# Two-layer attention on one core: the residual update moved to the next even block, four units between the layers, both group means in odd blocks

## The chip, the cores and the metric

The kernel runs on one core of a Trainium2 chip. The metric is the device time of one execution in microseconds (us), from the first to the last instruction. The engines are named as in the profile: PE is TensorE, the matrix engine (PEld is its weight load), DVE is VectorE, ACT is ScalarE, POOL is GpSimd, SP is SyncE, which here only issues DMA transfers. [...]

## The reference

Two layers, both of the same form, over x of shape (16, 256, 32, 32): a group norm, then attention with four heads over 1024 positions, then a residual.

```python
def layer(x, Wq, bq, Wk, bk, Wv, bv, rel_h, rel_w):     # heads 4, d 64, n 1024
    xf = gn(x).reshape(b, c, n)          # mean and variance over groups of the last axis
    q, k, v = proj(Wq, bq), proj(Wk, bk), proj(Wv, bv)
    sim  = einsum('bhdi,bhdj->bhij', q, k)
    qpos = einsum('hdi,bhdj->bhij', (rel_h + rel_w).reshape(heads, d, n), q)
    attn = softmax(sim + qpos, axis=-1)
    return x + einsum('bhdn,bhmn->bhdm', v, attn).reshape(b, c, w, h)
```

The norm of layer 1 reads the x that layer 0 has updated, so the two layers of one batch depend on each other; different batches do not.

## The kernel before

**Units and blocks.** A unit is one layer of one batch; there are 32, and the list `units` (L139 to L142) sets their order. Before the change the layer-1 unit of a batch follows its layer-0 unit by three to five places. A unit is cut into four blocks, by pair of heads `pr` (0, 1) and by half of the queries `half` (0, 1). In this text b0, b1, b2, b3 are the four blocks of a unit; b0 and b2 are **even** (`half` is 0), b1 and b3 are **odd**. There are 128 blocks, 31 units and the first two blocks of the last going through `block` (L621) and the last two through `block_without_pieces` (L747).

**One block.** For each of eight tiles j of 128 keys: DVE writes the position term of the scores into PSUM (`seed`, L343), PE adds the products of k and q to it (`scores`, L379), ACT takes the exponential into `p` in SBUF (L388). DVE adds up the tiles 0 to 6 of `p` into `acc` (`add_up`, L397 and L399); tile 7 is added by an accumulating DMA from POOL's queue (`add_last`, L430). PE multiplies `p` with the values in two stretches (`attend`, L413) into `po`, and ACT copies `po` to `od` (`take_out`, L488). Between the score tiles PE makes the projections for the coming blocks (`prepare`, L262, L292, L320). PSUM holds four buffers of this size, whose roles are in `ring`; a seed needs the buffer that an earlier exponential, copy or mean has been read out of.

**Tokens.** A product of two stretches has a dependence between them that PE is told of through POOL: POOL waits for the last matmul of the first stretch, writes `token` (L163), and PE's second stretch waits for it. `x.word()` places this write in POOL's queue.

**Softmax sums.** The `acc` of a block is folded by DMA: `add_last`, then `fold` (L435, POOL's queue, 256 KB accumulating), then `stack_up` (L444, SP's queue), then `fold_again` (L451, POOL). PE sums the stack at the end of the next even block (L463), ACT copies the sums out (L478), and two transfers on SP's queue bring them to `den_all` (L484).

**The residual of a pair.** `reciprocals` (L515) waits for `den_all`, takes the reciprocal on DVE (L522), writes it to DRAM (`rd`, L524) and reads it back spread over 64 partitions each (`rden`, L529), both on SP's queue. `finish` (L534) multiplies `od` by `rden` (L541), adds bias and x (L543), both on DVE, and in layer 1 stores x (L545). Before the change both stand in the same odd block: `reciprocals` after score tile 4, `finish` behind the first stretch of `attend` and ahead of the seeds 1 to 3 of the block that follows. `load_x` (two transfers of 512 KB for a later batch, L106) stands near the start of b3, ahead of both on SP's queue.

**The norm of a later unit.** ACT takes the group sums of unit u+2 (`norm_sums`, 16 instructions), then PE the mean over rows (`norm_mean`, L207), then ACT the sums of squares (`norm_squares`, 16), PE their mean (`norm_var`), POOL the reciprocal root (L231), and in the next unit ACT normalises (`norm_apply`, 16). Before the change the sums lie in b1 and b2, the mean in b2, the squares in b2 and b3, the second mean in b3, and the normalisation in b0 (15) and b1 (1). A mean needs a PSUM buffer, `f1`, zeroed by DVE (L199) and read by ACT before the next seed can use it.

Of the kernel before, what the change touches and what calls it, by code (L numbers as in the profile page):

```python
# [19 lines left out]
G = 16  # L20
# [32 lines left out]
def fast_path(ctx, tc, sh, x, layers, out, W, den_all, token, good, flag):  # L53
# [49 lines left out]
    def load_x(b):  # L103
        xt[b] = xpool.tile([P, CC, N], F32, tag="x", name=f"x_{b}")
        for cc in range(CC):
            nc.sync.dma_start(xt[b][:, cc, :], flat(x[b, cc * P : (cc + 1) * P]))  # L106
# [29 lines left out]
            nc.scalar.copy(w.rearrange("p a c -> p (a c)"), raw_t.pop((l, part)))  # L136


    units = [(b, 0) for b in range(3)]  # L139
    for b in range(3, B):  # L140
        units += [(b - 3, 1), (b, 0)]
    units += [(b, 1) for b in range(B - 3, B)]  # L142
    NU = len(units)
    ks, qs, abt, vts, xns = {}, {}, {}, {}, {}
# [46 lines left out]
    def norm_sums(u, gs):  # L191
        if u not in reds:
            reds[u] = small.tile([P, G], F32, tag="red", name=f"red_{u}")
        for g in gs:
            of_group(u, g, AF.Identity, reds[u])
# [26 lines left out]
    def norm_squares(u, gs):  # L222
        for g in gs:
            of_group(u, g, AF.Square, sums[u], bias=negs[u][:, g : g + 1])
# [14 lines left out]
    def norm_apply(u, gs):  # L239
        rstd, shift = rss[u]  # L240
        for g in gs:
            nc.scalar.activation(  # L242
                grouped(xns[u], g),
                grouped(xt[units[u][0]], g),
                AF.Identity,
                bias=shift[:, g : g + 1],
                scale=rstd[:, g : g + 1],
            )
# [142 lines left out]
    def add_up(blk, j):  # L391
        u, pr, half = blk
        if j == 0:
            return
        if j == 1:
            accs[blk] = apool.tile([P, 2, HALF], F32, tag="acc", name=f"acc_{u}_{pr}_{half}")
            nc.vector.tensor_tensor(accs[blk], probs[blk, 0], probs[blk, 1], ALU.add)  # L397
        else:
            nc.vector.tensor_tensor(accs[blk], accs[blk], probs[blk, j], ALU.add)  # L399
# [221 lines left out]
    def block(n):  # L621
        blk = blocks[n]
        u, b = divmod(n, BPU)
        half = blk[2]
        before = blocks[n - 3][:2] if half == 1 and n > 2 else None
        after = blocks[n + 1] if n + 1 < len(blocks) else None
        previous = blocks[n - 1] if n > 0 else None
        one, two = u + 1 < NU, u + 2 < NU

        pieces = u + 1 < NU or b < 2  # L630
        if u + 1 == NU and b == 1:
            widen(u, 1)
        f0, f1, f2, f3 = ring
        folded = n - 1 < FOLDED
        if not pieces:
            return block_without_pieces(n, half)

        if previous:
            add_up(previous, 6)
            if folded:  # L640
                add_last(previous)
            else:
                add_up(previous, 7)
        for j in range(1, 4):
            scores(blk, j)
        if b == 3 and u + 3 < NU and units[u + 3][0] not in xt:
            load_x(units[u + 3][0])
        (first, first_out), (second, second_out) = prepare(u, b)
        first(0)
        if b == 0 and one:  # L650
            norm_apply(u + 1, range(0, 1))
        if b == 2 and two:
            norm_sums(u + 2, range(8, 11))
        if b == 3 and two:
            norm_squares(u + 2, range(6, 9))
        seed(blk, 4, f1)
        scores(blk, 4)
        add_up(blk, 1)
        if before:
            reciprocals(*before)  # L660
        if b == 0 and one:
            norm_apply(u + 1, range(1, 5))
        if b == 1 and one:
            norm_apply(u + 1, range(15, G))
        if b == 2 and two:
            norm_sums(u + 2, range(11, G))
        if b == 3 and two:
            norm_squares(u + 2, range(9, 11))
        second(0)
        if half == 1:  # L670
            second_out()
        first.word()
        if previous and folded:
            fold(previous)
            stack_up(previous)
        first(1)
        first_out()
        seed(blk, 5, f0)
        scores(blk, 5)
        add_up(blk, 2)  # L680
        if half == 0:
            second.word()
            if previous and folded:
                fold_again(previous)
            second(1)
            second_out()
        seed(blk, 6, f1)
        scores(blk, 6)
        if half == 0:
            ring[2:] = f3, f2  # L690
        seed(blk, 7, ring[2])
        scores(blk, 7)
        add_up(blk, 3)
        add_up(blk, 4)

        if after:
            seed(after, 0, f0)
        if n in check:
            next(checks)
        if b == 0 and one:  # L700
            norm_apply(u + 1, range(5, 10))
        if b == 3 and two:
            norm_squares(u + 2, range(11, G))
        po = psum2(ring[3], f"po_{n}")
        values_of_p = attend(blk, po)
        values_of_p(0)
        if two and b >= 2:
            mean, mean_out = (norm_mean if b == 2 else norm_var)(u + 2, zeroed(f1, f"pm_{n}"))
            mean(0)
        if after:  # L710
            scores(after, 0)
        values_of_p.word()
        if two and b >= 2:
            mean(1)
        if previous and folded and half == 1:
            fold_again(previous)
        if two and b >= 2:
            mean_out()
        add_up(blk, 5)
        if before:  # L720
            finish(*before)
        if after:
            for j in range(1, 4):
                seed(after, j, ring[j % 3])
        if b == 0 and one:
            norm_apply(u + 1, range(10, 15))
        if b == 1 and two:
            norm_sums(u + 2, range(0, 8))
        if b == 2 and two:
            norm_squares(u + 2, range(0, 6))  # L730
        values_of_p(1)
        if half == 1:
            take_out(blk, po)
            pos[n] = po
            return
        if n > 1:
            sums_of_pair(*blocks[n - 2][:2], po)
        take_out(blk, po, n > 1)
# [8 lines left out]
    def block_without_pieces(n, half):  # L747

        blk = blocks[n]
        u, pr, _ = blk  # L750
        f0, f1, f2, f3 = ring
        before = blocks[n - 2][:2] if half == 0 else (u, pr)
        first = index[before + (0,)]
        if half == 0:
            add_up(blocks[n - 1], 6)
        add_up(blocks[n - 1], 7)
        for j in range(1, 4):
            scores(blk, j)
        sums_of_p(blocks[first:n], pos[n - 1])
        keep_sums(outs[before], pos[n - 1], first, n - first)  # L760
        add_up(blk, 1)
        seed(blk, 7, f2)
        add_up(blk, 2)
        add_up(blk, 3)
        for j, tag in ((4, f1), (5, f0), (6, f1)):
            scores(blk, j, tag)
        reciprocals(*before, n - first)
        scores(blk, 7)
        add_up(blk, 4)
        if half == 0:  # L770
            seed(blocks[n + 1], 0, f0)
        po = pos[n] = psum2(f3, f"po_{n}")
        values_of_p = attend(blk, po)
        values_of_p(0)
        if half == 0:
            scores(blocks[n + 1], 0)
        if half == 0:
            seed(blocks[n + 1], 1, f1)
            seed(blocks[n + 1], 2, f2)
        add_up(blk, 5)  # L780
        if half == 0:
            seed(blocks[n + 1], 3, f0)
        add_up(blk, 6)
        if half == 0:
            finish(*before)
            values_of_p(1)
            take_out(blk, po)
            return
        add_up(blk, 7)
        acc = accs.pop(blk)  # L790
        pd = psum2(f0, "pd")
        sums_on_rows(acc, pd)
        values_of_p(1)
        finish_half(u, pr, 0, outs[u, pr][:, 0, :], rdens[u, pr][:, :HALF])
        rden = rdens[u, pr][:, HALF:]
        nc.vector.reciprocal(rden, pd[:, 0, :])
        pd = psum2(f2, "pd_columns")[:, 0, : 2 * HALF // P]
        sums_on_columns(acc, pd)
        finish_half(u, pr, 1, po[:, :, :QUART], rden)
        list(in_range(flatden[:, 8 * checked : 8 * n], 1))  # L800
        list(in_range(pd, 2))
        nc.vector.tensor_reduce(good[:, 3:4], good[:, 0:3], AX.X, ALU.min)
        pc = psum2(f1, "pc")[0:1, 0, 0:1]
        nc.tensor.matmul(pc, good[:, 3:4], W.ones[:, 0:1], start=True, stop=True)
        nc.vector.tensor_copy(flag, pc)
# [410 lines left out]
```

## Time and profile before

Three runs took 2679.92, 2682.69 and 2690.53 us; the median is 2682.69 us. The profiled execution has a span of 2682.0 us at a granted TensorE clock of 0.994.

| group of instructions | count | mean ns | what it is |
|---|---|---|---|
| DVE L343 | 1018 | 1228 | seed of one score tile |
| DVE L399, L397 | 644, 128 | 1218 | adding one tile to `acc` |
| DVE L541, L543 | 63, 63 | 1221, 1285 | the two halves of `finish` |
| ACT L388 | 1024 | 1117 | exponential of one tile |
| ACT L187 of `x` | 480 | 309 | one group's sum |
| ACT L187 of `x,neg` | 498 | 410 | one group's squares |
| ACT L242 | 496 | 496 | normalising one group |
| POOL L430 to landing | 124 | 4.7 us | tile 7 added by DMA, 512 KB |
| POOL L435 to landing | 124 | 3.6 us | `fold`, 256 KB |

The busy times say which engine is full on the average; the waits say which other engine or transfer an engine stood still for; the timeline, which lists the instructions in order of time, says where in a block it happened. A bracket such as [3.77 <-DMA rden<-rd] gives the idle time of that engine just before the instruction and what ended it.

The length of a block can be read off the timeline of ACT: it is the distance from the start of one block's exponential of tile 1 to the next block's. Over the units 2 to 28:

| block | mean us | shortest us |
|---|---|---|
| b0 | 22.29 | 21.21 |
| b1 | 18.83 | 18.04 |
| b2 | 21.76 | 21.50 |
| b3 | 19.94 | 18.52 |
| a unit | 82.82 | |

The first block's mark is at 33.52 us and the last block's at 2654.44 us, so 127 block lengths make up 2620.92 us of the span.

### The profile page before, as it was taken

How to read it: one execution, taken by the hardware profiler on the slowest of the kernel's cores; microseconds unless marked ns; L12 is line 12 of the kernel's file. 1: busy time of each engine (PE TensorE's matmuls, PEld its weight loads, DVE VectorE, ACT ScalarE, POOL GpSimd, SP SyncE). 2: the span in 40 equal slices, each digit the busy share in tenths (PEclk: the TensorE clock that was granted, in tenths of full speed). 3: DMA queues.
4: the chain of work that ended last, by engine and by line, in shares of the span. 5: the costliest groups of instructions: out<-in, count | busy, mean ns of one | idle time of the engine just before them, and what ended most of it. 6: DMA issues, size and time to landing. Idle time of an engine off the chain costs nothing.

```text
span 2682.0 us, 86789 instructions
## 1 busy us (share of the span) xinstructions
PE 2595.6 (97%) x37970; PEld 1410.4 (53%) x37970; DVE 2261.4 (84%) x2076; ACT 1986.3 (74%) x3996; POOL 565.7 (21%) x949
## 2 busy tenths in 40 slices
PE   8999999999999999999999999999999999999998
PEld 4555455554555555555545555455554555555555
DVE  7888888888888888888888888888888888889888
ACT  6777777777777777777777778777786777777754
POOL 1221222212222122222222221222212222122210
PEclk9999999999999999999999999999999999999999
DMA  3343343433434334343343333433334333333331
GB/s 88 59 83 64 70 90 70 92 68 69 97 67 90 75 59 103 69 85 75 70 91 71 83 75 79 84 69 80 81 75 85 66 82 81 70 75 73 79 75 46
DMA packets 93994, 205.30 MB, mean 77 GB/s; under 512 B 35880, under 2 KB 37416, under 8 KB 93608
## 3 DMA queue, kind: packets, MB, share of 16 engines
q0 software_dynamic: 39680, 113.80, 25.2%
q1 hardware_dynamic: 53928, 85.89, 11.5%
q8 instruction: 299, 4.90, 0.8%
q14 instruction: 87, 0.71, 0.1%
HBM read 51.78 MB, written 17.30 MB: 26 GB/s over the span
## 4 chain that ended last, share of the span: by engine, by line
PE 61%; DMA 16%; DVE 10%; issue 5%; ACT 4%; POOL 2%; SPq 1%; DVEq 0%; POOLq 0%
PE po L413 26%; PE ps L379 19%; PE pq L262 7%; DMA den_all<-od 6%; DVE ps L343 5%; PE pk L262 4%; PE pv L292 4%; DMA rd<-r 4%; DMA rden<-rd 4%; ACT p L388 2%; DVE acc L399 1%; ACT od L488 1%; DVE acc L397 1%; ACT junk L187 1%; PE po L463 1%
## 5 line engine op out<-in xcount | busy, mean ns | idle before, releaser
L343 DVE TENSOR_TENSOR ps<-abt 128x1024 f32<-128x1024 f32 x1018 | 1225.8, 1228 | 317.3 <-ACT p L388 123.2
L388 ACT ACTIVATE p<-ps,shift 128x1024 f32<-128x1024 f32 x1024 | 1102.3, 1117 | 432.3 <-PE ps L379 304.3
L379 PE MATMUL ps<-q,k 64*64 64x512 f32 x8192 | 1033.3, 600 | 48.6 <-DVE ps L343 45.6
L413 PE MATMUL po<-p,v 64*64 64x256 f32 x16384 | 933.1, 376 | 2.4 <-POOL token L163 2.4
L413 PEld LDWEIGHTS po<-p,v 64*64 64x64 f32 x16384 | 658.7, 133 | 306.8 <-issue 58.8
L399 DVE TENSOR_TENSOR acc<-acc,p 128x1024 f32<-128x1024 f32 x644 | 784.4, 1218 | 5.3 <-ACT p L388 0.5
L379 PEld LDWEIGHTS ps<-q,k 64*64 64x64 f32 x8192 | 313.4, 133 | 480.9 <-DVE ps L343 258.4
L451 POOL DMA_DIRECT2D stack<-acc x248 | 195.2, 874 | 450.6 <-DMA stack<-acc 424.1
L262 PE MATMUL pq<-xn,Wq 64*64 64x512 f32 x2048 | 244.6, 593 | 9.6 <-POOL token L163 9.2
L292 PE MATMUL pv<-Wv,xn 64*64 64x256 f32 x4096 | 247.6, 376 | 0.5 <-DVE var L864 0.3
L262 PE MATMUL pk<-xn,Wk 64*64 64x512 f32 x2048 | 243.2, 590 | 4.7 <-POOL token L163 4.6
L430 POOL DMA_DIRECT2D acc<-p x124 | 111.9, 903 | 536.9 <-ACT p L388 360.6
L292 PEld LDWEIGHTS pv<-Wv,xn 64*64 64x64 f32 x4096 | 176.6, 134 | 84.1 <-issue 51.5
L242 ACT ACTIVATE xn<-x,nshift,rstd 128x128 f32<-128x128 f32 x496 | 210.3, 496 | 3.7 <-POOL nshift L233 3.6
L163 POOL MEMSET token<- 1x1 f32 x380 | 50.8, 134 | 704.2 <-PE po L413 474.5
L187 ACT ACTIVATE junk<-x,neg 128x128 f32<-128x128 f32 x498 | 196.9, 410 | 1.0
L435 POOL DMA_DIRECT2D acc<-acc x124 | 101.9, 822 | 396.8 <-DMA acc<-p 387.2
L262 PEld LDWEIGHTS pq<-xn,Wq 64*64 64x64 f32 x2048 | 76.9, 134 | 155.6 <-issue 119.1
L397 DVE TENSOR_TENSOR acc<-p,p 128x1024 f32<-128x1024 f32 x128 | 155.9, 1218 | 0.0
L187 ACT ACTIVATE junk<-x 128x128 f32<-128x128 f32 x480 | 144.5, 309 | 1.0 <-DVE x L543 1.0
L262 PEld LDWEIGHTS pk<-xn,Wk 64*64 64x64 f32 x2048 | 73.9, 133 | 132.0 <-issue 102.8
L488 ACT COPY od<-po 128x512 f32<-128x512 f32 x127 | 74.7, 589 | 75.0 <-PE po L413 75.0
(79 smaller groups left out, 1173.5 us busy)
## 6 DMA issues: line engine op xcount, KB each, us to landing
acc<-p POOLq DMA_DIRECT2D x124, 512.0 KB, 4.7
rden<-rd SPq DMA_DIRECT2D x126, 256.0 KB
acc<-acc POOLq DMA_DIRECT2D x124, 256.0 KB, 3.6
x<-in_x_dram SPq DMA_DIRECT2D x32, 512.0 KB
stack<-acc SPq DMA_DIRECT2D x248, 64.0 KB
stack<-acc POOLq DMA_DIRECT2D x248, 64.0 KB, 2.6
out_dram<-x SPq DMA_DIRECT2D x31, 512.0 KB
den_all<-od SPq DMA_DIRECT2D x124, 4.0 KB
```

The lines of the kernel that those rows point to most:

```text
L187: nc.scalar.activation(junk, grouped(xt[units[u][0]], g), func, accum_out=into[:, g : g + 1], **bias)
L242: nc.scalar.activation(grouped(xns[u], g), grouped(xt[units[u][0]], g), AF.Identity, bias=shift[:, g : g + 1], scale=rstd[:, g : g + 1],)
L262: yield nc.tensor.matmul(pk[c, nh, :], w[l][rs, cc, c0 : c0 + D], xns[u][rs, cc, nh * HALF : (nh + 1) * HALF], start=(t == 0 and cc == 0), ...
L292: yield nc.tensor.matmul(pv[c, a, i, :], xns[u][rs, cc, j0 : j0 + D], W.wv[l][rs, cc, :], start=(t == 0 and cc == 0 and i == 0), stop=(t = ...
L343: nc.vector.tensor_tensor(ps.rearrange("p h (w y) -> p h w y", y=H), ab[:, :, :H].unsqueeze(2).to_broadcast([P, 2, XH, H]), ab[:, :, H + h ...
L379: nc.tensor.matmul(ps[c, h, :], a[hs, j0 : j0 + D], b[hs, columns], start=bool(tag) and i == 0, stop=i == len(terms) - 1, skip_group_check ...
L388: nc.scalar.activation(p, ps, AF.Exp, bias=W.shift)
L397: nc.vector.tensor_tensor(accs[blk], probs[blk, 0], probs[blk, 1], ALU.add)
L399: nc.vector.tensor_tensor(accs[blk], accs[blk], probs[blk, j], ALU.add)
L413: yield nc.tensor.matmul(po[c, a, :QUART], vts[u][rs, j, c0 : c0 + D], p[rs, h, a * QUART : (a + 1) * QUART], start=(t == 0 and j == 0), s ...
L430: nc.gpsimd.dma_start(accs[blk], probs[blk, NT - 1], accum_op=ALU.add)
L451: nc.gpsimd.dma_start(stacks[u, pr][r0 : r0 + R, :], acc[R:D, h, :], accum_op=ALU.add)
```

## The change

`finish` leaves the odd block in which its `reciprocals` stands and goes to the next even block, ahead of the first stretch of `attend`. `reciprocals` stays in the odd block, but moves from behind tile 4 to behind tile 5. `load_x` moves behind both and behind `stack_up` in b3. In exchange DVE's sixth addition of an odd block moves from the next block's start to its own end. In even blocks the token write of the second projection moves ahead of `fold`.

Layer 1 of a batch may then not start as early, so the order of units is changed: four layer-0 units first, and at least four units between the layers of a batch. This lets the group sums of unit u+2 start in b0; the mean is then taken in b1 and that of the squares in b3, both odd, all 16 squares in b2, and the normalisation is split over b0 (9) and b1 (7). The purpose is to give the round trip of the reciprocals a block's time more, and to share the work of DVE and ACT out more evenly between even and odd blocks.

```diff
-    units = [(b, 0) for b in range(3)]
-    for b in range(3, B):
-        units += [(b - 3, 1), (b, 0)]
+    units = [(b, 0) for b in range(4)] + [(0, 1), (1, 1)]
+    for b in range(4, B - 1):
+        units += [(b, 0), (b - 2, 1)]
+    units.insert(-1, (B - 1, 0))
     units += [(b, 1) for b in range(B - 3, B)]
...
-        before = blocks[n - 3][:2] if half == 1 and n > 2 else None
+        summed = blocks[n - 3][:2] if half == 1 and n > 2 else None
+        before = blocks[n - 4][:2] if half == 0 and n > 3 else None
...
         if previous:
-            add_up(previous, 6)
+            if half == 1:
+                add_up(previous, 6)
...
-        if b == 3 and u + 3 < NU and units[u + 3][0] not in xt:
-            load_x(units[u + 3][0])
...
         add_up(blk, 1)
-        if before:
-            reciprocals(*before)
...
         first.word()
+        if half == 0:
+            second.word()
         if previous and folded:
             fold(previous)
-            stack_up(previous)
         first(1)
         first_out()
         seed(blk, 5, f0)
         scores(blk, 5)
+        if summed:
+            reciprocals(*summed)
+        if previous and folded:
+            stack_up(previous)
+            if half == 0:
+                fold_again(previous)
+        if b == 3 and u + 3 < NU and units[u + 3][0] not in xt:
+            load_x(units[u + 3][0])
         add_up(blk, 2)
         if half == 0:
-            second.word()
-            if previous and folded:
-                fold_again(previous)
             second(1)
...
         if after:
             seed(after, 0, f0)
+        if before:
+            finish(*before)
...
-        if two and b >= 2:
-            mean, mean_out = (norm_mean if b == 2 else norm_var)(u + 2, zeroed(f1, f"pm_{n}"))
+        if two and half == 1:
+            mean, mean_out = (norm_mean if b == 1 else norm_var)(u + 2, zeroed(f1, f"pm_{n}"))
...
         add_up(blk, 5)
-        if before:
-            finish(*before)
+        if half == 1:
+            add_up(blk, 6)
         if after:
             for j in range(1, 4):
                 seed(after, j, ring[j % 3])
```

The places of the norm's instructions in a block, by the count in each:

| | b0 | b1 | b2 | b3 |
|---|---|---|---|---|
| before | 15 normalising | 1 normalising, 8 sums | 8 sums, 6 squares | 10 squares |
| after | 9 normalising, 9 sums | 7 normalising, 7 sums | 16 squares | none |

In the last two blocks the residuals move on in the same way: the even one finishes the pair before the last but one, and the last block takes over one more `finish`, near its start.

More of the change, by code (lines that the diff above doesn't have):

```diff
@@ L651, in block @@
             norm_apply(u + 1, range(0, 1))
[L652 to L655, printed above, removed]
+        if b == 1 and two:
+            norm_sums(u + 2, range(9, 11))
         seed(blk, 4, f1)
@@ L658, in block @@
         add_up(blk, 1)
-        if before:
-            reciprocals(*before)
         if b == 0 and one:
             norm_apply(u + 1, range(1, 5))
-        if b == 1 and one:
-            norm_apply(u + 1, range(15, G))
+        if b == 1 and two:
+            norm_sums(u + 2, range(11, 12))
         if b == 2 and two:
-            norm_sums(u + 2, range(11, G))
-        if b == 3 and two:
-            norm_squares(u + 2, range(9, 11))
+            norm_squares(u + 2, range(0, 5))
         second(0)
@@ L700, in block @@
         if b == 0 and one:
-            norm_apply(u + 1, range(5, 10))
-        if b == 3 and two:
-            norm_squares(u + 2, range(11, G))
+            norm_apply(u + 1, range(5, 9))
+        if b == 0 and two:
+            norm_sums(u + 2, range(0, 2))
+        if b == 1 and two:
+            norm_sums(u + 2, range(12, G))
+        if b == 1 and one:
+            norm_apply(u + 1, range(9, 11))
+        if b == 2 and two:
+            norm_squares(u + 2, range(5, 11))
         po = psum2(ring[3], f"po_{n}")
@@ L712, in block @@
         values_of_p.word()
-        if two and b >= 2:
+        if two and half == 1:
             mean(1)
@@ L716, in block @@
             fold_again(previous)
-        if two and b >= 2:
+        if two and half == 1:
             mean_out()
         add_up(blk, 5)
-        if before:
-            finish(*before)
+        if half == 1:
+            add_up(blk, 6)
         if after:
@@ L724, in block @@
                 seed(after, j, ring[j % 3])
[L725 to L728, printed above, removed]
+        if b == 0 and two:
+            norm_sums(u + 2, range(2, 9))
+        if b == 1 and one:
+            norm_apply(u + 1, range(11, G))
         if b == 2 and two:
-            norm_squares(u + 2, range(0, 6))
+            norm_squares(u + 2, range(11, G))
         values_of_p(1)
@@ L751, in block_without_pieces @@
         f0, f1, f2, f3 = ring
[L752 to L755, printed above, removed]
+        summed = blocks[n - 2][:2] if half == 0 else (u, pr)
+        before = blocks[n - 4][:2] if half == 0 else blocks[n - 3][:2]
+        first = index[summed + (0,)]
         add_up(blocks[n - 1], 7)
@@ L759, in block_without_pieces @@
         sums_of_p(blocks[first:n], pos[n - 1])
-        keep_sums(outs[before], pos[n - 1], first, n - first)
+        keep_sums(outs[summed], pos[n - 1], first, n - first)
+        if half == 1:
+            finish(*before)
         add_up(blk, 1)
@@ L766, in block_without_pieces @@
             scores(blk, j, tag)
-        reciprocals(*before, n - first)
+        reciprocals(*summed, n - first)
         scores(blk, 7)
@@ L775, in block_without_pieces @@
         if half == 0:
+            finish(*before)
             scores(blocks[n + 1], 0)
@@ L784, in block_without_pieces @@
         if half == 0:
-            finish(*before)
             values_of_p(1)
```

## Prediction

> **What bounds the kernel now.** I read the busy shares first, then the waits, then the timeline of one unit.
>
> ```profile
> PE 2595.6 (97%) x37970; PEld 1410.4 (53%) x37970; DVE 2261.4 (84%) x2076; ACT 1986.3 (74%) x3996; POOL 565.7 (21%) x949
> ```
>
> PE is taken all the time and DVE has 16% left, so PE sets the pace and DVE is the first candidate to hold it up. That PE is 97% busy doesn't mean that only 3% can be gained: where PE is fed well, three score tiles take 2.75 us (timeline, 882.32), where their seeds come late the same 24 matmuls are shown as busy for 4.70 us (859.26). The block lengths measure this better. The shortest b0, b1, b2 and b3 add up to 21.21 + 18.04 + 21.50 + 18.52 = 79.27 us, the mean unit takes 82.82. So 3.55 us a unit, or 110 over 31 units, are stalls of some kind. The waits name them:
>
> ```profile
> DVE ps L343 <- ACT neg L217: 92.1, 30, 4.0
> ...
> DVE od L541 <- DMA rden<-rd: 53.6, 20, 4.5
> ...
> PEld pq L262 <- POOL token L163: 24.0, 25, 2.8
> ...
> DVE r L522 <- DMA den_all<-od: 22.1, 28, 1.7
> ...
> PEld pm L207 <- ACT junk L187: 15.5, 30, 0.5
> ```
>
> Columns: total us, times, longest. The largest is harmless: DVE waits 3 us in b2 for the buffer of the mean, but PE runs its second stretch meanwhile and goes on without a gap at 837.58. The second is not, as this timeline of one b3 shows:
>
> ```profile
> 839.67 0.90 SPq L106 DMA_DIRECT2D x<-in_x_dram  x2
> ...
> 842.52 0.33 SPq L524 DMA_DIRECT2D rd<-r  x1
> ...
> 849.13 1.16 SPq L529 DMA_DIRECT2D rden<-rd  x2
> ...
> 855.52 1.23 DVE L541 TENSOR_TENSOR od<-od,rden 128x1024 f32<-128x1024 f32 x1 [3.77 <-DMA rden<-rd]
> 856.78 1.28 DVE L543 SCALAR_TENSOR_TENSOR x<-od,bv,x 128x1024 f32<-128x1024 f32 x1
> 857.98 3.52 DVE L343 TENSOR_TENSOR ps<-abt 128x1024 f32<-128x1024 f32 x3
> ...
> 859.26 3.14 PE L379 MATMUL ps<-q,k 64*64 64x512 f32 x16 [2.85 <-DVE ps L343]
> ```
>
> A load of x goes out, the round trip of the reciprocals takes 842.5 to 855.5, 13 us, DVE stands at `finish`, the seeds behind it come late, and PE stops. Without a load (888.05) the round trip makes it in time for 897.12. In the 13 b3 from unit 1 to 25 that have the load (the odd units) the block takes 21.35 us on the mean, against 18.53 in the undisturbed ones.
>
> The third wait is in b0:
>
> ```profile
> 1027.52 0.93 POOL L430 DMA_DIRECT2D acc<-p  x1 [1.38 <-DVE acc L399]
> ...
> 1034.54 0.83 POOL L435 DMA_DIRECT2D acc<-acc  x1 [5.41 <-DMA acc<-p]
> 1035.06 0.33 POOL L163 MEMSET token<- 1x1 f32 x1
> ...
> 1035.44 1.09 PE L262 MATMUL pq<-xn,Wq 64*64 64x512 f32 x8 [1.35 <-POOL token L163]
> ```
>
> The token for PE stands in POOL's queue behind `fold`, and `fold` waits for `add_last` to land. PE's q projection was ready and waited for a memset.
>
> [...] the rows L399 and L541 show 1218 and 1221. Back to back they start 1.13 to 1.15 us apart in the timeline, so I count 1.14 each. [...] beside the load of 839.67 `fold` can go 8.9 us after its `add_last` (840.36 to 849.23), without one 4.9 (882.75 to 887.63).
>
> **The change, part by part.** No arithmetic is added or removed; only places change.
>
> 1. `finish` a block later. Its data has then landed 15 us and more before (a round trip of 9 us from 888, against a `finish` that comes in the second half of the next block), instead of up to 4.5 us late, and the 53.6 us of DVE waits vanish. What it is worth to PE: b3 with the load falls by 21.35 − 18.53 = 2.8 us, 13 times, **37 us**. The late seeds also start the next b0 late (b0 after such a b3 takes 22.66 us, after the others 21.87); that is part of item 2.
>
> 2. Tokens ahead of `fold`, and an earlier `add_last`: the sixth addition of an odd block no longer waits behind three seeds of the next. b0 should come from 22.29 to about its shortest, 21.25: 1.04 × 31 = **32 us**. Nothing queued behind loses: `fold` waits for `add_last` longer than for either product.
>
> 3. `reciprocals` behind tile 5. At 887.77 DVE stood 0.73 us for `den_all` between two seeds, and PE then waited for tile 6 (891.47). One seed, 1.14 us, now fills this; longest wait so far 1.7. b1 would go from 18.83 to 18.04, but it takes over the mean: eight tiny matmuls, and the four sums in front of it end about when they are needed (exponential of tile 7 ends some 1.7 us into the stretch, 4 × 0.30 us of sums, stretch 3.45). I take 18.4: 0.43 × 31 = **13 us**.
>
> 4. The means. b2 loses one: 21.76 to 21.35, **13 us**, most of which is jitter passed on from b3. b3 keeps one but no squares in front of it, so the 0.52 us that PE waits for ACT (15.5 in the list) go: 18.53 to 18.1, 0.43 × 31 = **13 us**.
>
> 5. DVE's load by block, at 1.14 us an operation: even 5 additions + 8 seeds + 2.4 for `finish` = 17.2 of 21.3 us; odd 7 additions + 8 seeds + 0.3 = 17.4 of 18.2. Before: 15.96 and 18.7. I followed the queue through a pair with the buffer releases: in even blocks the last seed ends 1.1 us before PE needs it; in odd ones, after the buffer of tile 1 is free at 2.3 us, seed 6 ends at 8.25 where PE comes for it at 8.6. It fits, barely. Cost 0; bounded above by one addition, 1.14 us, in each of 63 odd blocks, 72 us.
>
> 6. ACT, at the timeline's 0.41 us for a normalisation, 0.30 a sum, 0.40 a square: b0 6.15 to 6.4 us, b1 2.8 to 5.0, b2 4.8 to 6.4, b3 4.0 to 0. The additions in b1 and b2 lie beside the stretches of `attend`, where ACT waits 3.20 us (898.07) and 3.02 (833.94) for PE. Cost 0; upper bound 4.05 us a unit.
>
> 7. `load_x` now runs across the end of b3; before, it stretched the `add_last` of the same block, and the next is 7 us away. Free, or up to the 1.2 us left when `add_last` lands 3.8 us later (8.5 us, its median in the odd units' b3, against 4.7) and the slack of `fold_again` before the next token (2.6 us at 877.9) is used up.
>
> 8. The order of units by itself computes the same. The last block gets a `finish`: 2.4 us of DVE under at least 10 us of PE work; I take +1.5.
>
> Sum, by block lengths, which also take in the small jitter of b3 in even units (18.88 on the mean): a unit at 21.25 + 18.4 + 21.35 + 18.1 = 79.1 us. Such sums never quite come in, since the queue of item 5 has half a microsecond of play; I add 0.6. 31 units at 79.7 and three blocks at 57.9 make 2528.6 us in place of 2620.9: −92.3 + 1.5, from 2682.7 to **2592**.
>
> **The rivals.**
>
> *A, the DMA contention only moves.* The store of x now goes out at the end of even blocks, just ahead of `den_all`, and the load just ahead of b0's `add_last`. For it: the round trip above shows how much a load can stretch others. Against: it has its 7 us. Price: item 7's 1.2 × 12, and a `den_all` 0.4 us too late in 62 odd blocks: 39 us, **2631**.
>
> *B, DVE becomes the bound in odd blocks.* For it: 17.4 of 18.2 us. Against: b1 had 18.7 us of DVE before and did 18.04 when nothing was late. Price 72 us: **2664**.
>
> *C, ACT pays.* The added norm work in b0 to b2 delays the exponentials and thus the buffers for the seeds, and what leaves b3 gains nothing: +4.05 us a unit against a gain of 3.1, × 31 = +29: **2712**. Against: the 3 us gaps of item 6.
>
> **How the numbers follow.** Forecast 0.70, A 0.16, B 0.08, C 0.06. Low end: no allowance and both odd blocks at 18.04 give 78.7 a unit, 2560; high end: A and a little more, 2634. Outside lie B, C and a little of the rest. Faster by over 0.5% (under 2669): the forecast, A and most of B, 0.92; within 0.5% 0.03; slower 0.05.
>
> **What would show it.** L541 has no wait for `rden` left; pq and pk no longer wait for tokens behind L435; b3 of odd units is as short as that of even ones (under 18.5 us) and b0 under 21.6. B would show as PE waiting for L343 at tiles 6 and 7 of odd blocks with DVE free of waits; A as waits of L522 for `den_all` or of PE for tokens behind L451; C as L343 waiting for L388 for much more than 123 us. The forecast is wrong if the stalls of b0 stay although the tokens come early: then something else than POOL made them.

## The result, and the profile after

The changed kernel takes 2569.01 us (median of 4 runs, 2566.68 to 2572.34), the kernel before 2686.61 (4 runs, 2679.92 to 2692.4). The ratio is 0.9564, 95% interval 0.9535 to 0.9593: 4.4% or about 117 us faster. The forecast was 2592, its range 2560 to 2634.

The page of the changed kernel, its first part, to be held against the line of before in the prediction:

```profile
PE 2542.5 (99%) x37970; PEld 1634.3 (64%) x37970; DVE 2260.2 (88%) x2076; ACT 1980.4 (77%) x3996; POOL 567.8 (22%) x949
```

The counts in this line are the same, and DVE is busy for the same 2260 us; only the span around it has shrunk. The chain that ended last, by engine, says it better than PE's 97 and 99%. Before:

```profile
PE 61%; DMA 16%; DVE 10%; issue 5%; ACT 4%; POOL 2%; SPq 1%; DVEq 0%; POOLq 0%
```

After:

```profile
PE 91%; DMA 4%; DVE 2%; POOL 1%; issue 1%; ACT 0%; SPq 0%; POOLq 0%; DVEq 0%; ACTq 0%
```

Most of the 16% of DMA (13%) were the steps `den_all`, `rd` and `rden` of the reciprocals. After the change they are under 1% of the chain. By the waits of the changed kernel (total us, times, longest):

```profile
PEld po L414 <- POOL token L164: 29.3, 67, 2.6
...
DVE ps L344 <- ACT neg L218: 29.2, 30, 1.2
...
PE po L414 <- POOL token L164: 5.0, 4, 1.7
...
DVE r L523 <- DMA den_all<-od: 1.4, 1, 1.4
```

L541 of before is L542 here. It has no line, since it never waits for `rden`; pq and pk have no line for tokens; PE waits for seeds for 0.8 us in all. What PE still waits for, 5.0 us at a token in four places, comes up below. The block lengths, measured as before over the units 2 to 28:

| block | mean before | mean after | shortest after | forecast |
|---|---|---|---|---|
| b0 | 22.29 | 21.42 | 21.17 | 21.25 |
| b1 | 18.83 | 18.20 | 18.18 | 18.4 |
| b2 | 21.76 | 21.16 | 21.15 | 21.35 |
| b3 | 19.94 | 18.19 | 18.19 | 18.1 |
| a unit | 82.82 | 78.96 | | 79.1 |

b1, b2 and b3 now hardly vary, with a load or without, and in the units 1 to 30 the trace shows no wait of PE's in them. The last block, from its mark to the end, takes 28.7 us in place of 27.6.

### The profile page after: what moved, and what is told of

Its sections match the earlier page's. It is cut to its first block, busy times and chain, and to the rows that moved or that the text cites. A ratio compares the mean times of both kernels' runs of the same rounds, so it can differ in the third digit from the quotient of the medians.

```text
span 2568.4 us, 86849 instructions
## 1 busy us (share of the span) xinstructions
PE 2542.5 (99%) x37970; PEld 1634.3 (64%) x37970; DVE 2260.2 (88%) x2076; ACT 1980.4 (77%) x3996; POOL 567.8 (22%) x949
## 4 chain that ended last, share of the span: by engine, by line
PE 91%; DMA 4%; DVE 2%; POOL 1%; issue 1%; ACT 0%; SPq 0%; POOLq 0%; DVEq 0%; ACTq 0%
PE po L414 32%; PE ps L380 31%; PE pk L263 8%; PE pq L263 8%; PE pv L293 8%; PE pa L321 2%; DMA acc<-p 1%; PE po L464 1%; DMA stack<-acc 1%; DMA acc<-acc 1%; DVE ps L344 1%; POOL rstd L232 1%; POOL stack L452 0%; DVE acc L400 0%; PE pm L208 0%
## 5 line engine op out<-in xcount | busy, mean ns | idle before, releaser
L344 DVE TENSOR_TENSOR ps<-abt 128x1024 f32<-128x1024 f32 x1018 | 1221.1, 1227 | 275.8 <-ACT p L389 95.8
L380 PE MATMUL ps<-q,k 64*64 64x512 f32 x8192 | 1007.2, 590 | 0.9 <-DVE ps L344 0.8
L414 PEld LDWEIGHTS po<-p,v 64*64 64x64 f32 x16384 | 773.2, 133 | 195.8 <-issue 48.4
L380 PEld LDWEIGHTS ps<-q,k 64*64 64x64 f32 x8192 | 366.0, 133 | 342.0 <-issue 188.3
L452 POOL DMA_DIRECT2D stack<-acc x248 | 195.3, 880 | 410.8 <-DMA stack<-acc 393.3
L164 POOL MEMSET token<- 1x1 f32 x380 | 36.9, 97 | 947.3 <-PE pm L208 351.0
L293 PEld LDWEIGHTS pv<-Wv,xn 64*64 64x64 f32 x4096 | 189.1, 133 | 67.8 <-issue 45.9
L431 POOL DMA_DIRECT2D acc<-p x124 | 129.5, 1044 | 404.1 <-ACT p L389 216.3
L263 PEld LDWEIGHTS pq<-xn,Wq 64*64 64x64 f32 x2048 | 97.7, 134 | 123.1 <-issue 115.4
L263 PEld LDWEIGHTS pk<-xn,Wk 64*64 64x64 f32 x2048 | 92.2, 134 | 108.4 <-issue 108.4
L436 POOL DMA_DIRECT2D acc<-acc x124 | 101.9, 822 | 208.2 <-DMA acc<-p 187.9
```

The lines of the kernel that those rows point to most:

```text
L263: yield nc.tensor.matmul(pk[c, nh, :], w[l][rs, cc, c0 : c0 + D], xns[u][rs, cc, nh * HALF : (nh + 1) * HALF], start=(t == 0 and cc == 0), ...
L293: yield nc.tensor.matmul(pv[c, a, i, :], xns[u][rs, cc, j0 : j0 + D], W.wv[l][rs, cc, :], start=(t == 0 and cc == 0 and i == 0), stop=(t = ...
L344: nc.vector.tensor_tensor(ps.rearrange("p h (w y) -> p h w y", y=H), ab[:, :, :H].unsqueeze(2).to_broadcast([P, 2, XH, H]), ab[:, :, H + h ...
L380: nc.tensor.matmul(ps[c, h, :], a[hs, j0 : j0 + D], b[hs, columns], start=bool(tag) and i == 0, stop=i == len(terms) - 1, skip_group_check ...
L414: yield nc.tensor.matmul(po[c, a, :QUART], vts[u][rs, j, c0 : c0 + D], p[rs, h, a * QUART : (a + 1) * QUART], start=(t == 0 and j == 0), s ...
L431: nc.gpsimd.dma_start(accs[blk], probs[blk, NT - 1], accum_op=ALU.add)
```

## The experiments

The forecast held, but it was a sum of parts, and two of the parts can be wrong together without the sum showing it. So four edits were done on the kernel before (a1 to a4), and all but the order of units were taken back singly from the changed kernel (u1 to u6). The sixth addition, the reciprocals and the norm's places were only taken back, not done alone. Times are medians; ratios are against the kernel before on the same chip.

**The order of units alone (a1).** The edit is the first part of the diff.

> The kernel before with the new order of units alone. Theory (the order only makes room for the other edits): no change, within 0.3%, about 2683 us, b3 of the units with a load still near 21.3 us. Rival (the order itself takes a wait away, since the norm of a layer-1 unit no longer follows right behind the residual of its layer 0): 10 us or more less.

Measured: 2684.8 us, ratio 0.9990 (0.9978 to 1.0001). The b3 with a load stays long: 21.79 us over the 13 of them, which in the new order are those of the units 0, 3, 5 and so on to 23, and 24. The order only makes room.

**The late load alone (a2).**

```diff
-        if b == 3 and u + 3 < NU and units[u + 3][0] not in xt:
-            load_x(units[u + 3][0])
...
             fold(previous)
             stack_up(previous)
+        if b == 3 and u + 3 < NU and units[u + 3][0] not in xt:
+            load_x(units[u + 3][0])
```

> The kernel before with load_x alone moved behind stack_up in b3. Theory (the load stretches the round trip of the reciprocals, and DVE's finish stands for it): the waits of L541 fall from 53.6 us to under 10, b3 of odd units from 21.35 to under 19.2 us and b0 after it by about 0.7, 45 us less in all, some 2640. Rival (finish in the odd block is too early in any case, the load only adds to it): less than 15 us gained, over 2668, with waits for rden left in most blocks that have a load.

Measured: 2636.24 us, ratio 0.9816 (0.9794 to 0.9838), 49 us gained, two fifths of the whole by moving one statement. b3 of odd units falls from 21.35 to 18.58, b0 after it from 22.66 to 21.64, the waits of L541 to 14.7 us (18 times). The theory holds, except that the waits for `rden` did not fall under 10 us.

**The token alone (a3).**

```diff
         first.word()
+        if half == 0:
+            second.word()
...
         if half == 0:
-            second.word()
```

> The kernel before with the second projection's token alone moved ahead of fold in even blocks. Theory (PE's projection waits behind fold's wait for add_last): pq and pk wait no more for tokens, b0 falls from 22.29 to about 21.6, 20 us less, some 2663. Rival (the stalls of b0 come from late seeds, and the token's wait only fills time lost anyway): under 7 us, over 2676, b0 near 22.1.

Measured: 2673.57 us, ratio 0.9947 (0.9929 to 0.9965), 14 us. Between the two: the weight loads of pq and pk had waited 24.0 and 20.8 us for tokens and do so no more, but only 14 us come out; b0 is at 22.01 on the mean.

**finish alone, with the order (a4).** The edit is that of `summed` and `before` in the diff; all else stays.

> The kernel before with the new order and finish moved to the next even block, all else as before (reciprocals behind tile 4, load early, tokens behind fold, sixth addition at the next block's start, norm as before). Theory (finish is what couples the round trip to PE; a block's delay is enough whatever the load does): no wait for rden, b3 of odd units under 19 us, 50 us less, some 2633. Rival A (contention only moves: the load still stretches add_last and fold of b3, and tokens and folds of b0 are late): 25 us or less gained, over 2658. It also tells whether the parts add up: if this and the moved load each gain 45 or more, they remove the same loss.

Measured: 2682.37 us, ratio 0.9986 (0.9971 to 1.0002): no change, where 50 us were expected; rival A has it. `finish` waits for `rden` no more and b3 with a load is at 18.54, as the theory had it. But the b0 after it has gone from 22.66 to 25.26, and b2 from 21.76 to 22.33. So the 2.8 us gained in each of 13 b3 (37 us) are lost again in the b0 behind (2.6 us each, 34). Its waits name two new stalls (L200 is the memset of the mean's buffer, L234 the last step of the norm on POOL), and tokens at which PE itself stands longer (in the kernel before 9.2 us at pq and 0.2 at pv):

```profile
PEld pq L263 <- POOL token L164: 53.6, 30, 3.7
...
PEld pm L208 <- DVE pm L200: 37.8, 29, 2.3
...
ACT xn L243 <- POOL nshift L234: 37.3, 15, 6.2
PE pq L263 <- POOL token L164: 31.5, 17, 2.9
...
PE pv L293 <- POOL token L164: 11.5, 11, 4.3
```

The late tokens come back in u2, and the memset in u6.

**The early load back in the changed kernel (u2).** The edit of a2 the other way round.

> The changed kernel with load_x back near the start of b3. Theory (nothing near waits for the round trip any more): within 8 us of 2569, no wait for rden; b0's rare stalls may even vanish, as the load is over sooner. Rival (the load stretches add_last, fold and stack_up of b3, which delays POOL's root and with it the normalisation and add_last of b0): 20 us or more slower, b0 of units after a load over 22 us.

Measured: 2609.02 us, ratio 0.9703 (0.9682 to 0.9725), 40 us slower than the changed kernel. The rival holds. `finish` doesn't wait for `rden`, b3 stays at 18.2, and the 13 b0 behind a load take 24.77 us on the mean, the others 21.20. The timeline of one such b3 and of the start of the b0 behind it, lines of SP, POOL and ACT, and at the end the place where PE stops:

```profile
1141.47 0.91 SPq L106 DMA_DIRECT2D x<-in_x_dram  x2
1141.77 0.89 POOL L431 DMA_DIRECT2D acc<-p  x1 [6.69 <-ACT p L389]
...
1150.63 0.83 POOL L436 DMA_DIRECT2D acc<-acc  x1 [6.50 <-DMA acc<-p]
...
1156.16 1.18 SPq L445 DMA_DIRECT2D stack<-acc  x2
...
1159.79 0.77 POOL L452 DMA_DIRECT2D stack<-acc  x1 [5.97 <-DMA stack<-acc]
...
1162.12 4.11 POOL L232 TENSOR_TENSOR rstd<-var,mhalf 128x16 f32<-128x16 f32 x1
...
1166.57 0.50 ACT L243 ACTIVATE xn<-x,nshift,rstd 128x128 f32<-128x128 f32 x1 [4.64 <-POOL nshift L234]
...
1167.17 0.48 POOL L164 MEMSET token<- 1x1 f32 x2
...
1167.56 1.96 PE L293 MATMUL pv<-Wv,xn 64*64 64x256 f32 x32 [2.80 <-POOL token L164]
```

Read it downwards. The load goes out 0.3 us before `add_last` (L431), and `fold`, which waits for it to land, follows only 8.9 us later. `fold` (L436), `stack_up` (L445) and `fold_again` (L452) move back with it, and behind `fold_again` in POOL's queue stands the reciprocal root of the norm (L232), for which ACT waits 4.64 us. Behind the root stand the next `add_last` and the token for the second stretch of b0's first projection (1167.17), and there PE stops for 2.80 us. The root starts 3.3 us after the mark of this b0 (1158.80); an undisturbed one in the changed kernel starts 3.0 us before it (1212.83, mark at 1215.82). Over the whole of u2, PE stands 32.4 us at two kinds of token, the one just shown and the one of `attend` behind the next `fold_again`; in the changed kernel it is 5.0 us, all of the second kind:

```profile
PE pv L293 <- POOL token L164: 17.0, 10, 2.8
...
PE po L414 <- POOL token L164: 15.4, 11, 3.0
```

So the load had two victims, `finish` and POOL's queue. The kernel before showed mainly the first. By its timeline the stop of PE in b3 gave POOL the time that it needed: in the b0 at 860.42 the root started 2.0 us before the mark (858.39), and ACT did not wait for it. This fits a4, which took the first stall away and laid the second one open; no run tests it by itself.

**finish back in the odd block (u1).**

> The changed kernel (2569 us) with finish back in the odd block, behind the sixth addition, all else as changed. Theory (finish has two costs, its wait and its 2.4 us of DVE in front of the next seeds; the load is out of the way, so the first is small, but the second now comes on top of the sixth addition): seeds come about 1.2 us late after each odd block, b0 and b2 longer by that together with b1 and b3, 75 us more, some 2645. Rival (only the wait for rden mattered): under 15 us more, under 2585.

Measured: 2643.5 us, ratio 0.984 (0.982 to 0.9859), 74 us slower. The theory's 75 is met, and the waits show that it is not the data:

```profile
PE ps L380 <- DVE ps L344: 31.7, 62, 1.4
...
DVE od L542 <- DMA rden<-rd: 1.3, 3, 0.8
```

`rden` is late by 1.3 us in all, but at all 62 starts of an even block behind an odd one PE waits for seeds; these stand behind the sixth addition and `finish`. The waits come to 31.7 of the 74 us; the rest shows in the block lengths alone. All four blocks are 0.3 to 0.8 us longer (21.75, 18.98, 21.73, 18.94). So in the final arrangement `finish` is worth its place as 2.4 us of DVE work, not as a consumer of a transfer.

**The norm and its means back (u6).** The places of the table in the section on the change, with the means in b2 and b3.

> The changed kernel with the norm's instructions and means where they were (means in b2 and b3, squares in b2 and b3, normalisation in b0 with one in b1). Theory (the squares right in front of the second mean cost PE 0.5 us in b3, and b2 now has finish and a mean): 15 to 30 us more, b3 near 18.6, b2 near 21.4, some 2590. Rival (the norm's places don't matter for PE, only room for finish was needed): under 7 us more.

Measured: 2613.02 us, ratio 0.9731 (0.97 to 0.9762), 44 us slower, more than expected. b3 is at 18.51 as forecast (18.6); b2 is at 22.33 against 21.16. The timeline of one b2:

```profile
1207.74 1.22 DVE L542 TENSOR_TENSOR od<-od,rden 128x1024 f32<-128x1024 f32 x1
1208.99 1.28 DVE L544 SCALAR_TENSOR_TENSOR x<-od,bv,x 128x1024 f32<-128x1024 f32 x1
...
1210.22 1.25 DVE L400 TENSOR_TENSOR acc<-acc,p 128x1024 f32<-128x1024 f32 x1
1210.29 0.07 DVE L200 MEMSET pm<- 128x16 f32 x1
1210.41 0.14 PEld L208 LDWEIGHTS pm<-red,avg 64*64 64x64 f32 x2 [1.24 <-DVE pm L200]
```

A memset of 0.07 us that PE needs for the mean stands on DVE behind the 2.4 us of `finish`. With the two in this order, a mean and `finish` in one block make b2 1.17 us longer; this is what "both means in odd blocks" avoids. That the two can't share a block at all is not shown: no run put the memset ahead of `finish`, though in this timeline ACT had read tile 6 out of that buffer by 1207.62, before `finish` began.

**Three small edits back, singly (u3 the token, u4 the sixth addition, u5 the reciprocals) and together (u7).**

> The changed kernel with the second projection's token behind fold again in even blocks. Theory (add_last lands at 7 to 8.5 us into b0, fold's issue takes 0.9, and PE comes for the token at 9.4): about 0.5 us lost in each b0, little in b2, 10 to 20 us more, some 2584. Rival (with the earlier add_last there is room): no change, under 2575.

> The changed kernel with the sixth addition of an odd block at the start of the next even block again. Theory (it delays add_last, fold and fold_again of even blocks by about 4 us, and the token of attend stands behind fold_again in POOL's queue): b0 grows by 1.5 us or so to 22.7, b2 by under 0.5, 30 to 60 us more, some 2615. Rival (there is slack in the fold chain, and DVE has room in even blocks): under 8 us more.

> The changed kernel with reciprocals behind tile 4 again. Theory (den_all lands about 5.4 us into an odd block, and DVE, with 17.4 of 18.2 us of work there, stands for it between two seeds): waits of L523 for den_all 20 us or more, odd blocks 0.3 to 0.5 us longer, 20 to 30 us more, some 2594. Rival (DVE catches up before tile 6): under 7 us more, odd blocks at 18.2.

> The changed kernel with three of its small edits taken back together: the second token behind fold, the sixth addition of an odd block at the next block's start, reciprocals behind tile 4. What stays is the order of units, finish in the even block, the norm's places and the late load. Theory (the three act on the same chain of fold transfers and POOL's queue, and each had slack only because the other two were there): more than the sum of the single effects, which were +3, +12 and +6 us, namely b0 over 22.3 us and 2600 or more. Rival (they are independent and small): about 2590, b0 under 22.

Measured: u3 2571.5 us, ratio 0.9565 (0.9542 to 0.9587), no change; u4 2581.0, 0.9596 (0.9563 to 0.9629), and u5 2574.94, 0.9573 (0.9542 to 0.9603), neither clear of the changed kernel. The b0 of u4 is at 21.81 on the mean, far from the 22.7 expected; in u5 the waits for `den_all` come to 4.3 us, not 20. All three theories priced too much. Together (u7) they cost 26 us: 2595.31, 0.9661 (0.9627 to 0.9695), against 21 for the sum. That decides little between the two theories: b0 (21.62) is where the rival had it. More than in the single runs (at most 18.24 and 21.25), b1 and b2 grow too (18.46, 21.42), and the waits for `den_all` (12.0 us) and for tokens before pq (25.5) are back.

**A version that beats both (v1).** What is left over in the changed kernel are a few b0 of 22.9 to 23.2 us (units 16, 22, 27). One of them, from its timeline:

```profile
1310.70 1.57 POOL L452 DMA_DIRECT2D stack<-acc  x2 [6.93 <-DMA stack<-acc]
...
1311.70 0.60 POOL L164 MEMSET token<- 1x1 f32 x1
...
1312.36 3.68 PE L414 MATMUL po<-p,v 64*64 64x256 f32 x64 [1.53 <-POOL token L164]
```

The token stands behind `fold_again`, which is late because `add_last` had to stand behind the root at the end of b3. In the units 16 and 22, which follow a load, the root itself is late (it starts 1.2 us before the mark of b0 and 0.3 us after it, not 3.0 before). In unit 27, which follows no load, it is on time, and `add_last` took 6.0 us to land, where 4.7 is the median in b0. v1 issues an odd block's `add_last` at that block's own end, ahead of the root:

```diff
         if half == 1:
             add_up(blk, 6)
+            if n < FOLDED:
+                add_last(blk)
+        if two and b == 3:
+            norm_root(u + 2)          # rstd and nshift, taken out of norm_var
```

> The changed kernel with the odd block's add_last at its own end, in POOL's queue ahead of the reciprocal root of the norm (4.3 us of POOL), not behind it. Theory (the few longer b0, 22.9 to 23.2 us in units 16, 22 and 27, come from add_last starting behind the root, so that fold_again holds the token of attend): b0 at 21.18 throughout, 6 us less, some 2563. Rival (they come from slow transfers, or the root now comes too late for the normalisation): no change, or slower with normalisation waiting for POOL.

Measured: 2562.96 us (2562.86 to 2563.78), ratio 0.9534 (0.951 to 0.9558), as expected. b0 is at 21.21. Its interval overlaps that of the changed kernel, so the 6 us rest on the medians and on the trace, where the wait that was 5.0 us is now:

```profile
PE po L419 <- POOL token L164: 0.2, 1, 0.2
```

## Why the prediction was right, and where it was not

The sum was right: 79.1 us a unit were worked out, 78.96 measured. The remaining 23 us between 2592 and 2569 are mostly the allowance of 0.6 us a unit (18.6 us), which wasn't needed. But part of this is luck. Each block was set near its shortest length, so the sum had to come in once nearly all stalls were gone, whichever edit removed them; and an edit that the prediction gave no gain, the late load, was in the change. The errors of the four blocks (b0 and b3 longer by 0.17 and 0.09, b1 and b2 shorter by 0.20 and 0.19) also cancel in part.

- *Step 1, finish a block later, 37 us:* right that b3 with a load falls to its undisturbed length, and `finish` alone does that (18.54, a4); wrong that the 37 us then come out. `finish` alone gave about 4 us (a4), not clear of nothing, the late load alone 49 (a2). The step looked at one consumer of the slow transfers. The 8.9 us for `add_last` beside a load were quoted in the prediction, but what hangs behind them was not followed to POOL's root and to the tokens behind it. Rival A named the direction (the contention only moves).
- *Step 2, tokens and an earlier add_last, 32 us:* b0 did come down by 0.87 us or 27. The token gave 14 alone and nothing at the end (a3, u3); the late load alone brings b0 to 21.70 on the mean.
- *Step 3, reciprocals, 13 us:* b1 fell by 0.63 us (20), but taking the reciprocals back brings back only about 6 (u5). With `finish` alone gone from the odd block (a4), b1 is already at 18.42. One seed more in front of L523 had little to hide.
- *Step 4, the means, 26 us:* right in direction, too small. With the norm's places as before, b2 with `finish` in it is 1.17 us longer (u6), a collision that the step didn't see.
- *Step 5, DVE's load:* right. Odd blocks hold 17.4 of 18.2 us by the prediction's count, and PE waits for seeds 0.8 us in all. u1 shows how near the edge this is: 2.4 us more cost 74.
- *Step 6, ACT at nothing:* right. L344 waits for exponentials 95.8 us, before 123.2.
- *Step 7, the load across the end of b3, "free":* this is the term that was mis-sized most. Of the edits done alone it gains most, 49 us (40 by taking it back), and it was entered as a possible cost. The small loss that was named for it, a token behind `fold_again`, did occur, in the b0 of the units 16 and 22 with about 1.8 us each; the third long b0, of unit 27, follows no load.
- *Step 8:* the order is worth nothing (a1), and the last block took 1.1 us more, forecast 1.5.

Singly taken back, the load, the norm and `finish` cost 40 + 44 + 74 = 158 us, more than the whole change gained: they depend on each other. `finish` in the even block is worth 74 us with the load late and the means odd, and gained nothing with the load early and a mean in its block (a4). Which of the two alone would do for it was not run.

## What to carry to other kernels

A transfer that makes one consumer late can make others late too: here the early load cost `finish` most of its 53.6 us of waits for `rden` in the kernel before (14.7 with the load late, a2), and with `finish` out of the way PE stood 32.4 us at POOL's tokens against 5.0 (u2). Before moving the consumer, follow every transfer that is under way in that stretch, and what stands behind it in each queue, to the end. A stall can shelter another, as a4 suggests (37 us gained in the b3, 34 lost again in the b0 behind): when a wait is removed and the time stays, look in the next block for what that wait had covered. And when work moves from one block to another, look for the smallest instruction queued behind its new place: a 0.07 us memset behind the 2.4 us of `finish` held TensorE's weight load for 1.24 us (u6, at 1210.41) and went with a b2 that was 1.17 us longer.

## What the runs showed of the hardware

The prediction had nothing on the clock. After the stall of 2.85 us in the block shown there, TensorE ran at half clock for 3.4 us, from 860.28 on. So the 4.70 us that the prediction read there as matmuls whose seeds come late were in part a slower clock. The windows of the kernel before, with busy times and counts of the engines, then PEclk (the granted clock, 1.00 is full speed), the share of DMA and GB/s:

```profile
860.30:863.60 3.30, 3.23 (x20) 0.99 (x20) 3.30 (x4) 2.23 (x2) 3.00 (x3) 0.50 0.17 29
863.70:880.00 16.30, 16.30 (x236) 8.22 (x232) 13.13 (x13) 12.58 (x19) 2.76 (x7) 1.00 0.39 66
```

The trace of before has seven such stretches of 3.4 us inside the span, each worth at most about 1.7 us, an estimate that takes half of it as lost. The changed kernel has none before its last 7 us, and its mean clock is 0.999 against 0.994; that of the late load alone (a2) is 0.999 too. The length of the gap ahead doesn't decide alone. In the kernel before, the gap of 2.85 us (to 859.26) and one of 2.01 us (to 361.23) were followed by such a stretch, the second from 361.93 on; one of 3.05 us (to 1687.45) was not, and the clock stayed at 1.00 up to 1694. In the changed kernel it stayed at 1.00 after the gap of 1.53 us (1312.36 above). What else decides is open. So at most some 12 us of the 117, and of the 49 of a2, can be clock that was lost beside the stalls, by the same estimate seven times 1.7.
